# First terms of a depthwise sum on ScalarE instead of VectorE, with VectorE's other sums in the reverse order

## Chip, cores, metric

One core of one Trainium2 chip. The metric is the device time of one execution in microseconds (us), the median of several. A ratio is the mean time of one kernel's fast runs over that of the other kernel's fast runs of the same rounds, so it is not quite the ratio of the medians quoted beside it. Intervals are 95%.

## The reference

Input `x` is 2 x 256 x 128 x 128 in fp32. Layer 0 normalises it by groups and adds a block whose expensive part are three branches of a deformable depthwise 3x3 convolution (dilations 1, 9 and 12): each of nine taps reads the image at a bilinearly interpolated place, and the taps are summed with one weight per channel and tap. Then come LayerNorm, GELU, a 1x1 convolution and an MLP. Layer 1 is a group norm and a 3x3 convolution with ternary weights.

```python
def _deform_dw(x, offset, w, pad, dil):
    ...
    sampled = _bilinear(x, py, px)
    wk = w.reshape(C, K)
    return jnp.einsum('bckhw,ck->bchw', sampled, wk)
...
def _branch(x, w_off, w_def, lw, lb, pad, dil):
    off = _conv(x, w_off, pad, dil)
    y = _deform_dw(x, off, w_def, pad, dil)
    return jax.nn.gelu(_ln2d(y, lw, lb), approximate=False)
```

## The kernel before

The changed stage is sampling. One *unit* is two input rows of one branch; each unit has two halves of 128 channels, and I call such a half a *sample*. For a sample:

- TensorE multiplies 14 tiles `xs` of the padded image with the interpolation weights `A`, two tiles per PSUM buffer `pm` (four buffers).
- ScalarE copies each `pm` into `ev` (two buffers), for all nine taps.
- VectorE builds `A` of the next but one unit from `hy` and `hx` (loads of 384 KB each, three buffers), and adds `weight x ev` of each tap to rows of a ring, one ring for each branch. The first tap that touches a row writes it (the *first term*, `tensor_scalar`), the others add to it (the *sums*, `scalar_tensor_tensor`).

A *row of taps* is the three taps kx = 0, -1, 1 of one ky. The sample's two input rows feed ring rows y - ky x dilation, so the rows of taps of one unit write different ring rows in the two wide branches, and overlapping ones at dilation 1. Nearly all ring rows are begun by ky = -1 (752 of the 788 first terms). Between the samples the work on finished rows (transposes, LayerNorm, GELU, MLP: the *tail*) is interleaved in a fixed program order.

```python
def accumulate(u, c, ev, ky):                       # one row of taps
    ...
    for kx in (0, -1, 1):
        ...
            dst = ring[:, c, y % n_ring : y % n_ring + j - i, x0:x1]
            src = ev[:, tap * RI + i : tap * RI + j, u0 : u0 + x1 - x0]
            if new:
                ...                                 # frees the ring rows' last owner
                pin(nc.vector.tensor_scalar(dst, src, w, None, ALU.mult))
                begun.update((b, br, c, y + m) for m in range(j - i))
            else:
                pin(nc.vector.scalar_tensor_tensor(dst, src, w, dst, ALU.mult, ALU.add))
            i = j

def sample(u, c):
    ...
    ev = pool.tile([P, 9 * RI, NT * CI], F32, name="ev", tag="ev", bufs=2)
    for T in range(0, NT, 2):
        ...
        pm = psum.tile([P, 2, 256], F32, name="pm", tag="pm", bufs=4)
        for j in range(2):
            pin(nc.tensor.matmul(pm[:, j, 0:n], lhsT=xts[b, Rt][T + j][...], rhs=A[...], ...))
        pin(nc.scalar.copy(ev[...], pm[...]))
    if c == KC - 1:
        prepare(u + 2)                              # builds A of unit u + 2, loads for u + 3
    for ky in kys:                                  # -1, 0, 1
        accumulate(u, c, ev, ky)
```

## Time and profile before

| | before |
|---|---|
| median of 4 runs | 7882.2 us (7873.1 to 7889.1) |
| stages in the profile | first stage to 980 us, sampling to 6670 us, last stage to 7903 us |
| VectorE first terms | 788 instructions, 748 of them 128x256 |
| VectorE sums | 6272 instructions |

The lines are in the prediction below. Two ways of counting are added here, because the experiments use them. In steady stretches the program repeats every 12 samples; I take the time from the first copy of sample 100 to that of sample 364 of the first image, and between the same places of the second (484 to 772 of all 796), 46 repeats together. It is 88.21 us for a repeat in this profile and 88.35 us in a second one taken later. And the records of the granted clock show TensorE at half its clock in pieces of 3413 ns and more; in the steady stretches (1450 to 3600 and 4250 to 6400 us) there are 68 such pieces, 78 in the second profile.

### The profile page before, as it was taken

To read this page: it belongs to the slowest core of one execution; us is meant where nothing else is said; L and a number is where in the kernel's file an instruction comes from. 1 tells how busy PE (TensorE), PEld (TensorE's weight loads), DVE (VectorE), ACT (ScalarE), POOL (GpSimd) and SP (SyncE) were. 2 spreads that over 40 slices of the span, in tenths; PEclk is the share of its full clock that TensorE was granted. 3 is DMA by queue.
4 is the path that set the end of the run, shared out by engine and by line. 5 is a ranking of instruction groups with operands and counts; after the bars stand their busy time and mean duration, and the time that the engine had idled before them with its cause. 6 is when DMAs were issued, how large, how long until landed. Compare 5 with 4: busy or idle time off the path is not lost. (4 is left out here: it accounts for less than half of the span.)

```text
span 7903.1 us, 115440 instructions
## 1 busy us (share of the span) xinstructions
PE 7101.1 (90%) x37984; PEld 5421.9 (69%) x37984; DVE 6400.1 (81%) x13680; ACT 4514.7 (57%) x9350; POOL 715.1 (9%) x1292
## 2 busy tenths in 40 slices
PE   5999887899999999899988989999998999699999
PEld 2555577777887777777777777877787777344444
DVE  6666578888999889988688898898889986577776
ACT  1344355666666666667655666666666666333232
POOL 0000000111111111111100111111111111000000
PEclk9999889999999999999999999999999999799999
DMA  8767799999999999998689999999999995222121
GB/s 280 215 187 195 187 229 243 235 247 246 244 240 249 242 243 241 246 243 224 192 233 243 239 248 245 243 240 245 249 240 244 243 242 162 74 74 78 63 82 48
DMA packets 1011327, 1652.66 MB, mean 209 GB/s; under 512 B 120800, under 2 KB 573200, under 8 KB 1006360
## 3 DMA queue, kind: packets, MB, share of 16 engines
q1 hardware_dynamic: 993304, 1611.57, 76.3%
q10 hardware_dynamic: 17408, 33.56, 1.3%
q8 instruction: 304, 4.98, 0.3%
q14 instruction: 311, 2.55, 0.1%
HBM read 1376.69 MB, written 268.09 MB: 208 GB/s over the span
## 5 line engine op out<-in xcount | busy, mean ns | idle before, releaser
L759 PE MATMUL pm<-A,xs 128*128 128x180 f32 (+2 forms) x22288 | 3638.8, 319 | 578.6 <-ACT ev L768 551.2
L759 PEld LDWEIGHTS pm<-A,xs 128*128 128x128 f32 x22288 | 3431.7, 196 | 791.6 <-ACT ev L768 652.0
L768 ACT COPY ev<-pm 128x360 f32<-128x360 f32 (+2 forms) x5572 | 2283.3, 456 | 1517.3 <-DVE ring L733 751.3
L733 DVE SCALAR_TENSOR_TENSOR ring<-ev,defw,ring 128x256 f32<-128x256 f32 (+5 forms) x6272 | 2786.9, 463 | 212.5 <-ACT ev L768 43.2
L689 DVE TENSOR_TENSOR A<-hy,hx 128x768 f32<-128x768 f32 x1130 | 1018.7, 946 | 343.5 <-DMA hx<-hats 170.7
L487 ACT ACTIVATE T<-T,rs 128x256 f32<-128x256 f32 x1280 | 663.8, 595 | 3.3 <-POOL rs L483 3.2
L1083 PE MATMUL pc<-cring,signs 128*128 128x512 bf16 x2304 | 522.8, 386 | 56.1 <-DVE signs L971 23.6
L480 POOL TENSOR_SCALAR rs<-mv 128x4 f32<-128x4 f32 x320 | 108.0, 337 | 5108.0 <-DVE mv L478 4133.9
L1083 PE MATMUL pc<-cring,sums 128*128 128x512 bf16 x2304 | 510.3, 380 | 0.0
L446 PE MATMUL hp<-T,w 128*128 128x512 f32 x1024 | 490.7, 604 | 7.8 <-ACT T L565 7.8
L476 DVE BATCH_NORM_STATS2 st<-T 128x6 f32<-128x256 f32 x1280 | 446.9, 412 | 23.2 <-ACT T L468 23.2
L203 PE MATMUL pz<-wz,xa 128*128 128x486 f32 x1024 | 461.2, 584 | 4.3 <-DVE zr L210 4.3
L1083 PEld LDWEIGHTS <-signs 128*128 128x128 bf16 x2304 | 227.5, 99 | 340.7 <-issue 46.2
L446 PE MATMUL h<-hT,w 128*128 128x512 f32 x1024 | 460.1, 592 | 0.0
L1083 PEld LDWEIGHTS <-sums 128*128 128x128 bf16 x2304 | 225.4, 98 | 274.4 <-DVE sums L1143 0.2
L499 PEld LDWEIGHTS zc<-ident,T 128*128 128x128 f32 x2560 | 342.0, 156 | 98.2 <-issue 61.5
L515 ACT ACTIVATE T<-zc,bb,bw 128x512 f32<-128x512 f32 x384 | 278.5, 779 | 227.8 <-PE zc L499 226.8
L499 PE MATMUL zc<-ident,T 128*128 128x128 f32 x2560 | 384.5, 297 | 19.6 <-ACT T L487 14.1
L1067 ACT CAST cring<-D 128x2048 bf16<-128x2048 f32 x128 | 243.3, 1902 | 222.9 <-PE pc L1083 152.2
L482 POOL TENSOR_TENSOR rs<-rs,mhalf 128x4 f32<-128x4 f32 x320 | 369.6, 1155 | 0.0
L468 ACT COPY T<-tp 128x512 f32<-128x512 f32 x640 | 345.2, 599 | 38.0 <-PE tp L466 37.3
L1091 ACT ACTIVATE o<-xl,l1b 128x1024 f32<-128x1024 f32 x64 | 73.5, 1149 | 506.9 <-DMA out_x<-o 431.7
(120 smaller groups left out, 5768.7 us busy)
## 6 DMA issues: line engine op xcount, KB each, us to landing
hy<-hats SPq DMA_DIRECT2D x1114, 384.0 KB, 6.4
hx<-hats SPq DMA_DIRECT2D x1114, 384.0 KB, 7.3
xs<-table SPq DMA_DIRECT2D x1876, 128.0 KB, 4.4
g12d<-T SPq DMA_DIRECT2D x128, 512.0 KB, 7.1
other<-g12d SPq DMA_DIRECT2D x128, 512.0 KB, 10.1
hats<-hb SPq DMA_DIRECT2D x192, 240.0 KB, 4.3
hats<-hb SPq DMA_DIRECT2D x192, 192.0 KB, 3.3
xl<-x1d SPq DMA_DIRECT2D x56, 640.0 KB, 4.1
```

The costliest lines, as they stand in the source:

```text
L203: nc.tensor.matmul(pz[:, 0:NZ], lhsT=xt[:, c, r, :], rhs=k["wz"][:, c, :], start=c == 0, stop=c == KC - 1,)
L446: nc.tensor.matmul(out, lhsT=w, rhs=v, start=i == 0, stop=i == n - 1)
L468: nc.scalar.copy(Tv[:, 2 * h : 2 * h + 2, :].rearrange("p j c -> p (j c)"), tp)
L476: pin(nc.vector.bn_stats(st[:, j, :], Tv[:, j, :]))
L482: nc.gpsimd.tensor_tensor(rs[:, 0, :], rs[:, 0, :], mhalf[:, 0:NB4], ALU.pow)
L487: nc.scalar.activation(Tv[:, j, :], Tv[:, j, :], AF.Identity, scale=rs[:, 0, j : j + 1], bias=rs[:, 1, j : j + 1],)
L499: nc.tensor.transpose(zc[:, j * P : (j + 1) * P], Tv[:, j, c * P : (c + 1) * P], ident)
L689: nc.vector.tensor_tensor(dst, hy[:, i0:i1].rearrange("p i t w -> p t i w"), hx[:, i0:i1].rearrange("p i t w -> p t i w"), ALU.mult,)
L733: nc.vector.scalar_tensor_tensor(dst, src, w, dst, ALU.mult, ALU.add)
L759: nc.tensor.matmul(pm[:, j, 0:n], lhsT=xts[b, Rt][T + j][:, c * P : (c + 1) * P], rhs=A[:, m0:m1, AO + (T + j) * CI : AO + (T + j + 1) * C ...
L768: nc.scalar.copy(ev[:, m0:m1, T * CI : (T + 2) * CI].rearrange("p m (t j) -> p t m j", j=CI), pm[:, :, 0:n].rearrange("p t (m j) -> p t m ...
L1083: nc.tensor.matmul(pc[:, bank, :], lhsT=w[:, m * P : (m + 1) * P], rhs=xc[:, i, k, t * JC : (t + 1) * JC, kx : kx + W], start=j == 0, stop ...
```

## The change

The intent is to take work off VectorE, which shares the stage's bound, and give it to ScalarE, which is idle for a third of it. As the sums of ky = -1 now need what another engine writes, they go last, so that ScalarE is done by then.

```diff
-        def accumulate(u, c, ev, ky):
+        def accumulate(u, c, ev, kys):
...
+            sums = {ky: [] for ky in kys}
+            for ky in kys:
...
-                        pin(nc.vector.tensor_scalar(dst, src, w, None, ALU.mult))
+                            pin(nc.scalar.mul(dst, src, w))
...
-                        pin(
-                            nc.vector.scalar_tensor_tensor(
-                                dst, src, w, dst, ALU.mult, ALU.add
-                            )
-                        )
+                            sums[ky].append((dst, src, w))
...
+            for ky in reversed(kys):
+                for dst, src, w in sums[ky]:
+                    pin(nc.vector.scalar_tensor_tensor(dst, src, w, dst, ALU.mult, ALU.add))
...
-            for ky in kys:
-                accumulate(u, c, ev, ky)
+            accumulate(u, c, ev, kys)
```

More of the change, by code (lines that the diff above doesn't have):

```diff
@@ L695, in build @@
             )
-        def accumulate(u, c, ev, ky):
+        def accumulate(u, c, ev, kys):
             b, Rt, br = units[u]
             dil = DILS[br]
-            i0, i1 = valid(Rt, br, ky)
             ring = k["rings"][br]
             n_ring = RINGS[br]
-            for kx in (0, -1, 1):
-                tap = (ky + 1) * 3 + kx + 1
-                x0, x1 = max(0, -REACH - kx * dil), min(W, W + REACH - kx * dil)
-                u0 = x0 + kx * dil + REACH
-                w = defw[:, c, br * 9 + tap : br * 9 + tap + 1]
-                i = i0
-                while i < i1:
-                    y = Rt * RI - REACH - ky * dil + i
-                    new = (b, br, c, y) not in begun
-                    j = i + 1
-                    while (
-                        j < i1
-                        and (y + j - i) % n_ring
-                        and ((b, br, c, y + j - i) not in begun) == new
-                    ):
-                        j += 1
-                    dst = ring[:, c, y % n_ring : y % n_ring + j - i, x0:x1]
-                    src = ev[:, tap * RI + i : tap * RI + j, u0 : u0 + x1 - x0]
-                    if new:
-                        assert kx == 0
-                        for m in range(y, y + j - i):
-                            owner = owners.get((br, m % n_ring // R))
-                            while owner and owner != (b, br, m // R) and owner not in tail.read:
-                                tail.advance()
-                            owners[br, m % n_ring // R] = b, br, m // R
-                        pin(nc.vector.tensor_scalar(dst, src, w, None, ALU.mult))
-                        begun.update((b, br, c, y + m) for m in range(j - i))
-                    else:
-                        pin(
-                            nc.vector.scalar_tensor_tensor(
-                                dst, src, w, dst, ALU.mult, ALU.add
-                            )
-                        )
-                    i = j
@@ new lines, in accumulate @@
+            sums = {ky: [] for ky in kys}
+            for ky in kys:
+                i0, i1 = valid(Rt, br, ky)
+                for kx in (0, -1, 1):
+                    tap = (ky + 1) * 3 + kx + 1
+                    x0, x1 = max(0, -REACH - kx * dil), min(W, W + REACH - kx * dil)
+                    u0 = x0 + kx * dil + REACH
+                    w = defw[:, c, br * 9 + tap : br * 9 + tap + 1]
+                    i = i0
+                    while i < i1:
+                        y = Rt * RI - REACH - ky * dil + i
+                        new = (b, br, c, y) not in begun
+                        j = i + 1
+                        while (
+                            j < i1
+                            and (y + j - i) % n_ring
+                            and ((b, br, c, y + j - i) not in begun) == new
+                        ):
+                            j += 1
+                        dst = ring[:, c, y % n_ring : y % n_ring + j - i, x0:x1]
+                        src = ev[:, tap * RI + i : tap * RI + j, u0 : u0 + x1 - x0]
+                        if new:
+                            assert kx == 0
+                            for m in range(y, y + j - i):
+                                owner = owners.get((br, m % n_ring // R))
+                                while owner and owner != (b, br, m // R) and owner not in tail.read:
+                                    tail.advance()
+                                owners[br, m % n_ring // R] = b, br, m // R
+                            pin(nc.scalar.mul(dst, src, w))
+                            begun.update((b, br, c, y + m) for m in range(j - i))
+                        else:
+                            sums[ky].append((dst, src, w))
+                        i = j
```

## The prediction

> **What bounds the kernel now.** I read the page first, then the table of stretches, the waits, the timeline of one repeat, and the groups by shape. The page's busy times and slices (198 us each) show that the stage in which all changed lines run, sampling, lasts from slice 5 to slice 33, about 1000 to 6670 us.
>
> ```profile
> PE 7101.1 (90%) x37984; PEld 5421.9 (69%) x37984; DVE 6400.1 (81%) x13680; ACT 4514.7 (57%) x9350; POOL 715.1 (9%) x1292
> ...
> PE   5999887899999999899988989999998999699999
> ...
> DVE  6666578888999889988688898898889986577776
> ACT  1344355666666666667655666666666666333232
> ...
> DMA  8767799999999999998689999999999995222121
> ```
>
> TensorE, VectorE and the DMA engines all stand near nine tenths there, ScalarE near seven. The table of stretches gives figures (columns: length, busy us and count of PE, PEld, DVE, ACT, POOL, granted clock, DMA share, GB/s), first for a steady stretch, then for the first rows of the second image:
>
> ```profile
> 5000.00:6000.00 1000.00, 920.07 (x5137) 791.23 (x5136) 895.31 (x2041) 679.88 (x1462) 129.02 (x228) 0.97 0.94 244
> ...
> 4100.00:4200.00 100.00, 80.03 (x495) 75.97 (x494) 85.79 (x184) 57.02 (x131) 5.83 (x12) 0.95 0.98 250
> ```
>
> Three resources within 3% of each other cannot all be the bound at once: they take turns. The waits of the sampling stage (us in total, times, longest) say how they hand over.
>
> ```profile
> PE pm L759 <- ACT ev L768: 550.5, 300, 6.5
> ...
> ACT ev L768 <- DVE ring L733: 751.3, 343, 8.0
> ACT ev L768 <- PE pm L759: 443.1, 352, 3.7
> ...
> DVE A L689 <- DMA hx<-hats: 158.6, 115, 6.2
> DVE A L689 <- PE pm L759: 142.5, 68, 8.4
> DVE ring L729 <- ACT ev L768: 105.6, 74, 4.3
> ```
>
> Read together: `ev` has two buffers, so ScalarE may not copy sample s out of PSUM before VectorE has finished the sums of sample s-2; while it waits, four `pm` banks fill and TensorE stops. That is the 550 us. In other places VectorE waits for TensorE or a load.
>
> The steady part repeats every 88.7 us (12 samples: 6 units of two channel halves). In one repeat, 5024.9 to 5113.6, TensorE has just four gaps, and these are them in the timeline (start, us, what, then [idle before <- releaser]):
>
> ```profile
> 5028.95 2.10 PE L759 MATMUL pm<-A,xs 128*128 128x180 f32 x12 [0.43 <-ACT ev L768]
> ...
> 5058.25 3.78 PE L759 MATMUL pm<-A,xs 128*128 128x180 f32 x12 [3.30 <-ACT ev L768]
> ...
> 5070.91 2.10 PE L759 MATMUL pm<-A,xs 128*128 128x180 f32 x12 [0.43 <-ACT ev L768]
> ...
> 5079.32 3.58 PE L759 MATMUL pm<-A,xs 128*128 128x180 f32 x12 [2.99 <-ACT ev L768]
> ```
>
> ScalarE's own rows before the last three show waits of 3.63, 1.85 and 2.37 us for VectorE's sums. So VectorE sets the end only from about 5050 (where it starts building `A` just as TensorE finishes with the old one) to 5079. From 5079 until the next stall near 5147 TensorE runs on with no more than 0.43 us lost at one place, and VectorE's first terms there (eight of twelve) are hidden behind it. The four at 5053.11, 5057.54, 5065.96 and 5074.56 are exposed.
>
> **What the skill says.** "VectorE: DVE Perf Modes", section on the perf-mode tier table: an fp32 `tensor_scalar` in SBUF gets 2x, a two-tensor op 1x. The trace agrees: for the same 256 elements 342 ns against 483 ns, a difference of 141 ns where 128 cycles saved at the page's 0.96 GHz are 133. So the change takes VectorE's cheapest ring write away, not its dearest. "ScalarE: Activation LUTs", section "What ACT_TABLE_LOAD costs": 186 ns + 0.833 ns per element, about 93 ns more per [128,1] operand. The trace agrees: two operands and 256 elements give 585 against 595 ns (L487); one operand and 512 elements give 706 against 716 (L538). For the new form, one operand and 256 elements, it gives 492; I add the same 10 ns and a little for waiting on the engine's own last copy: 520 ns, an estimate from that page. "Perfetto Trace Analysis", section on Scalar/DVE operations: if VectorE is saturated, moving work to ScalarE may pay. VectorE's 895 of 1000 us against ScalarE's 680 is that situation, but only for a third of each repeat.
>
> **The change part by part.** The groups by shape (count | busy us, mean ns | idle before):
>
> ```profile
> L768 ACT COPY ev<-pm 128x360 f32<-128x360 f32 x4788 | 2037.6, 472 | 1320.7 <-DVE ring L733 688.0 <-PE pm L759 388.8 <-PE hp L446 12.5
> L733 DVE SCALAR_TENSOR_TENSOR ring<-ev,defw,ring 128x256 f32<-128x256 f32 x2832 | 1366.7, 483 | 110.3 <-ACT ev L768 43.2
> ...
> L487 ACT ACTIVATE T<-T,rs 128x256 f32<-128x256 f32 x1280 | 663.8, 595 | 3.3 <-POOL rs L483 3.2
> ...
> L729 DVE TENSOR_SCALAR ring<-ev,defw 128x256 f32<-128x256 f32 x748 | 255.8, 342 | 113.0 <-ACT ev L768 112.6
> ```
>
> Removed: 788 first terms from VectorE (748 of them this wide). From the start of one to the start of the next sum is 0.38 us (5053.11 to 5053.49), so about 788 x 0.38 = 299 us of VectorE's queue. On the path are four per repeat: 4 x 0.38 = 1.5 us of 88.7, or 1.7%. Steady stretches are roughly 1450 to 3650 and 4300 to 6450 us, 4350 us together, hence 49 repeats: 49 x 1.5 = 74 us. At the start of each image I count nothing: between 4000 and 4300 VectorE stands 39 us waiting for `hx` and the DMA share is up to 0.98. At each image's end few rows are begun at all.
>
> Added: 788 x 0.52 = 410 us on ScalarE (4515 to about 4925). By the built programs' order each stands just after the seven copies of its sample and waits for nothing but these, so it falls into the time in which ScalarE waits for VectorE or TensorE next. In the stretch that counts these waits were 3.6, 1.9 and 2.4 us, and where TensorE leads 3.6 us before sample 5024.94. I put 0 on the path. No activation table load is added: three before and after.
>
> Moved: the sums of the lowest row of taps (`ky` = -1, to which nearly all first terms belong) come last. With three or six other sums of some 0.48 us first, VectorE has 1.4 to 2.9 us before it needs the 0.52 us write. The removed 0.38 us is thus not replaced by a wait. The sums keep number and sizes, and TensorE's order is instruction for instruction the same. Sum: 7885 - 74, say **7812 us**, 0.9% less.
>
> **The rivals.** (1) VectorE is the bound throughout: all 299 us come off, 7586 us. For it: 89.5% busy and 751 us of ScalarE waiting for it. Against: its own waits of over 500 us in this stage, and TensorE without gaps for two thirds of a repeat. (2) The DMA takes it back: share 0.94 and 243 GB/s against at most 250 GB/s in stretches where loads are the visible wait. A repeat shorter by 1.7% needs 247. For it: `hx` already ends 115 waits, and buffers that come free sooner only queue the loads sooner. Then a third to all of the 74 us goes: 7835 to 7885. (3) ScalarE becomes the bound: it would rise from 68 to about 75% in steady stretches; where it interleaves tail work with copies, 0.5 us per sample could delay TensorE. If half the samples lost 0.2 us, 796 x 0.5 x 0.2 = 80 us would cancel the gain: about 7890. Against: TensorE's gaps from ScalarE all begin with VectorE or lie behind a 3.6 us idle time of ScalarE.
>
> **Range and chances.** The mechanism removes at most what lies on the path, so 74 is nearer a ceiling than a middle of the steady part; the start of the images, and repeats in which more first terms are exposed than in the one I read, can add some 40 to 60 us. Down to 7750 on that side. On the other, rivals 2 and 3 reach 7875. Faster by over 2% means under 7728, twice my saving: 5%. Slower by over 2% would need ScalarE to become the path: 2%.
>
> **What would show it.** Right: VectorE's first-term group gone; a ScalarE group of 788 at 500 to 540 ns; VectorE busy near 6130; ScalarE near 4920; the repeat about 87.2 us; TensorE's wait for `ev` down by 60 to 100 us; no wait of the sums for the first terms. Wrong: the wait for `hx` grown by some 70 us (rival 2), TensorE's wait for `ev` grown while ScalarE's for VectorE shrank (rival 3), or TensorE's wait nearly halved (rival 1). A new write much over 520 ns, or a repeat in which VectorE leads for longer than 29 us, would make the number wrong.

## The result, and the profile after

The changed kernel takes 7756.2 us (median of 4, 7735.4 to 7761.0) against 7882.2 us, ratio 0.984 [0.982, 0.986]: 126 us less. This is within the range (7750 to 7875), 6 us from its lower end, under the 2% of "faster", and 52 us more gain than the 74 us predicted.

The page's busy times of the changed kernel, then its row of the steady stretch (length, busy us and count of PE, PEld, DVE, ACT, POOL, clock, DMA share, GB/s):

```profile
PE 7065.1 (91%) x37984; PEld 5377.1 (69%) x37984; DVE 6136.4 (79%) x12892; ACT 4818.2 (62%) x10138; POOL 708.7 (9%) x1292
```

```profile
5000.00:6000.00 1000.00, 929.10 (x5308) 799.91 (x5308) 877.58 (x1960) 753.59 (x1656) 131.45 (x232) 0.98 0.96 250
```

VectorE lost 264 us and 788 instructions, ScalarE gained 304 us. In the steady thousand TensorE does 171 more matmul records in the same time (a product of the sampling is two records), VectorE is less busy, and the DMA moves 250 GB/s where it moved 244. The groups by shape (count | busy us, mean ns | idle before):

```profile
L740 DVE SCALAR_TENSOR_TENSOR ring<-ev,defw,ring 128x256 f32<-128x256 f32 x2832 | 1355.2, 480 | 248.7 <-ACT ev L771 174.2 <-DVE ring L740 0.9
...
L733 ACT ACTIVATE ring<-ev,defw 128x256 f32<-128x256 f32 x748 | 378.8, 509 | 23.6
```

The first term costs ScalarE 509 ns where it cost VectorE 342, and ScalarE hardly waits for it. The waits of the sampling stage, one fence for each engine (us, times, longest):

```profile
PE pm L762 <- ACT ev L771: 437.1, 276, 7.9
```

```profile
ACT ev L771 <- DVE ring L740: 461.3, 253, 8.7
ACT ev L771 <- PE pm L762: 393.8, 236, 5.3
```

```profile
DVE A L689 <- DMA hx<-hats: 227.0, 151, 7.3
DVE ring L740 <- ACT ev L771: 175.2, 89, 5.8
DVE A L689 <- PE pm L762: 139.2, 66, 5.8
...
DVE ring L740 <- ACT ring L733: 14.4, 9, 3.0
```

TensorE waits 113 us less, ScalarE waits 290 us less for VectorE, and VectorE waits more for loads and for ScalarE's copies (175.2 us where two lines of the kernel before had 105.6 and 32.9): it comes earlier. For the first terms themselves it waits 14 us. TensorE's gaps in one repeat (start, us, what, [idle before]):

```profile
4998.66 2.10 PE L762 MATMUL pm<-A,xs 128*128 128x180 f32 x12 [0.42 <-ACT ev L771]
...
5026.64 2.10 PE L762 MATMUL pm<-A,xs 128*128 128x180 f32 x12 [1.98 <-ACT ev L771]
...
5038.26 2.10 PE L762 MATMUL pm<-A,xs 128*128 128x180 f32 x12 [0.84 <-ACT ev L771]
...
5046.31 2.10 PE L762 MATMUL pm<-A,xs 128*128 128x180 f32 x12 [2.64 <-ACT ev L771]
```

The two large gaps stand at the same two samples of the repeat (the 8th and the 11th of twelve) as before, 2.0 and 2.6 us instead of 3.3 and 3.0. And something that I had overlooked before: behind them twelve records (six products) take 2.10 us, while in the kernel before they took 3.78 and 3.58 us behind the large gaps. The clock records show why: a half-clock piece of 3413 ns begins at 5058.47 us and one at 5078.95 us, and none in this repeat of the changed kernel. Where the gain arises, from the two profiles:

| part of sampling | before | after | gain |
|---|---|---|---|
| samples 0 to 100 (start of image 1) | 645.3 | 623.6 | 21.7 |
| 100 to 364, steady | 1945.0 | 1892.2 | 52.8 |
| 364 to 412 (end of image 1) | 326.9 | 331.2 | -4.3 |
| 412 to 484 (start of image 2) | 505.5 | 496.3 | 9.2 |
| 484 to 772, steady | 2112.6 | 2059.7 | 52.9 |
| 772 to 796 (end) | 153.2 | 153.0 | 0.2 |

The first stage, which the change doesn't touch, differs by 20 us between the two profiles; a second profile of the kernel before (below) lies between. That is spread, and not part of the table.

### The profile page after: what moved, and what is told of

It is laid out like the page before. It is cut to its first block, busy times and chain, and to the rows that moved or that the text cites. A ratio compares the mean times of both kernels' runs of the same rounds, so it can differ in the third digit from the quotient of the medians.

```text
span 7751.0 us, 115301 instructions
## 1 busy us (share of the span) xinstructions
PE 7065.1 (91%) x37984; PEld 5377.1 (69%) x37984; DVE 6136.4 (79%) x12892; ACT 4818.2 (62%) x10138; POOL 708.7 (9%) x1292
## 5 line engine op out<-in xcount | busy, mean ns | idle before, releaser
L740 DVE SCALAR_TENSOR_TENSOR ring<-ev,defw,ring 128x256 f32<-128x256 f32 (+3 forms) x6272 | 2774.5, 462 | 359.7 <-ACT ev L771 175.2
L771 ACT COPY ev<-pm 128x360 f32<-128x360 f32 (+2 forms) x5572 | 2235.8, 455 | 1131.6 <-DVE ring L740 462.9
L733 ACT ACTIVATE ring<-ev,defw 128x256 f32<-128x256 f32 (+1 forms) x788 | 392.2, 503 | 24.1
L499 PEld LDWEIGHTS zc<-ident,T 128*128 128x128 f32 x2560 | 325.9, 151 | 97.5 <-issue 61.5
L499 PE MATMUL zc<-ident,T 128*128 128x128 f32 x2560 | 368.7, 289 | 20.1 <-ACT T L487 13.9
```

Of the source, the lines that this page charges most:

```text
L499: nc.tensor.transpose(zc[:, j * P : (j + 1) * P], Tv[:, j, c * P : (c + 1) * P], ident)
L733: pin(nc.scalar.mul(dst, src, w))
L771: nc.scalar.copy(ev[:, m0:m1, T * CI : (T + 2) * CI].rearrange("p m (t j) -> p t m j", j=CI), pm[:, :, 0:n].rearrange("p t (m j) -> p t m ...
```

## The experiments

Eleven kernels ran (no run has the number e11). All results were correct except in the one made wrong. This table holds what the traces of all give; it is used below. *Block* is the time that VectorE takes for the first terms and sums of 12 samples, from the start of the first to the end of the last, as the sum of the median blocks of the three branches times four. *Repeat* is the mean of 46, *half-clock* the number of half-clock pieces in the steady stretches.

| kernel | ratio to before [95%] | block, us | repeat, us | half-clock |
|---|---|---|---|---|
| before (two profiles) | 1.001 [0.999, 1.002] (e8) | 51.3 | 88.21, 88.35 | 68, 78 |
| changed | 0.984 [0.982, 0.986] | 46.9 | 85.91 | 41 |
| e1 order only | 0.992 [0.990, 0.993] | 49.8 | 87.18 | 62 |
| e2 ScalarE only | 0.987 [0.985, 0.988] | 46.7 | 86.37 | 52 |
| e3 no first terms | 0.981 [0.980, 0.983] | 46.7 | 85.72 | 40 |
| e4 first terms twice on VectorE | 1.023 [1.021, 1.025] | 56.0 | 91.40 | 85 |
| e5 before, stalls filled | 0.997 [0.996, 0.999] | as before | 87.20 | 5 |
| e6 changed, stalls filled | 0.982 [0.981, 0.983] | as changed | 85.34 | 0 |
| e7 first terms twice on ScalarE | 0.988 [0.986, 0.989] | as changed | 86.00 | 35 |
| e9 before, sums spread | 0.967 [0.965, 0.969] | 42.8 | 84.12 | 29 |
| e10 changed, sums spread | 0.962 [0.960, 0.963] | 39.6 | 83.19 | 20 |
| e12 before, filled elsewhere | 1.005 [1.002, 1.008] | as before | 88.91 | 23 |

**e1: the order alone.** The first terms stay on VectorE.

```diff
-                            pin(nc.scalar.mul(dst, src, w))
+                            pin(nc.vector.tensor_scalar(dst, src, w, None, ALU.mult))
```

> The first terms stay on VectorE, only its sums run in the reverse order of rows of taps. My theory (the gain is VectorE time taken off the stretches in which VectorE leads, plus shorter TensorE stalls that less often end in a half-clock window): nothing is taken off VectorE, so the ratio to the kernel before is 0.998 to 1.002, VectorE stays near 6400 us busy and the half-clock windows in the steady stretches stay near 68. Rival (the order itself frees rows of the ring or shortens dependent sums): a part of the 1.6% is seen here, 0.995 or less.

Measured: 7829.2 us, ratio 0.992. My expectation was wrong and the rival's range came true: reversing the sums alone gives half of the gain, though not one instruction leaves VectorE. The timeline tells which of the rival's two reasons it was. A first term and the eight sums behind it, in the kernel before:

```profile
5037.82 0.35 DVE L729 TENSOR_SCALAR ring<-ev,defw 128x256 f32<-128x256 f32 x1
5038.20 3.77 DVE L733 SCALAR_TENSOR_TENSOR ring<-ev,defw,ring 128x238 f32<-128x238 f32 x8
```

and in e1:

```profile
5037.04 0.35 DVE L733 TENSOR_SCALAR ring<-ev,defw 128x256 f32<-128x256 f32 x1
5037.31 3.76 DVE L740 SCALAR_TENSOR_TENSOR ring<-ev,defw,ring 128x256 f32<-128x256 f32 x8
```

Before, the sum behind the first term adds to the rows that this has just written, and starts 0.38 us after it. In e1 it belongs to other rows and starts after 0.27 us, while the first term's 0.35 us are not over. The same is seen among the sums over two rows (about 250 elements, 0.47 to 0.48 us each): the median step between two starts is 0.38 to 0.40 us where the next one has other rows, and 0.50 to 0.52 us where it adds to the rows just written. So here an instruction starts some 0.08 us before the end of the one in front, but 0.03 us after it if it needs that one's result: about 0.12 us later. e1 removes one dependent neighbour per sample, 51.3 - 49.8 = 1.5 us per repeat, of which 1.1 us arrive in the time. I took this as the new theory and tested it in e9.

**e2: ScalarE alone.** The sums keep their order.

```diff
-            for ky in reversed(kys):
+            for ky in kys:
```

> The first terms go to ScalarE, but VectorE's sums keep the order of before, so the sums that need the first terms come first. My theory: where VectorE leads it is behind ScalarE by more than a sample, so the first term is there already; only where VectorE waits for ScalarE's copies (about once in 12 samples, where TensorE leads) does it wait some 0.5 us more. So 0.984 to 0.988 of before, almost the whole gain. Rival (the order is needed): a wait of 0.5 us takes the place of the removed 0.38 us in most samples, the ratio is 0.995 or more and VectorE's wait for ScalarE's first terms is over 100 us.

Measured: 7786.2 us, ratio 0.987, as expected within its range. VectorE's waits:

```profile
DVE A L689 <- DMA hx<-hats: 257.0, 161, 6.7
DVE ring L740 <- ACT ring L733: 180.3, 86, 6.2
...
DVE ring L740 <- ACT ev L771: 47.3, 18, 4.4
```

Of the rival, one sign came (a wait for first terms of over 100 us) and the other did not (a ratio of 0.995 or more): VectorE waits for first terms 86 times, about once or twice per repeat, not in all 796 samples, in places where the changed kernel waits 89 times for the copies in front of them (175 us). The sum of both waits is 227.6 us against 189.6. So the order's own purpose, to hide ScalarE's latency, is worth some 0.3% (0.987 against 0.984 in other rounds; 0.46 us per repeat). It also shows that the two parts do not add up: the order shortens a block by 1.5 us and the move by 4.7, but both together by 4.4, because without the first term there is no dependent neighbour left for the order to break up, and at dilation 1 the fourth sum now waits for both engines and starts 0.07 us later than in e3, which has no first terms.

**e3: no first terms anywhere** (wrong, the rings are cleared once).

```diff
-                            pin(nc.scalar.mul(dst, src, w))
...
+            for ring in k["rings"]:
+                nc.vector.memset(ring, 0.0)
```

> Wrong result on purpose: the first terms are left out on both engines (the ring is cleared once), all else as in the changed kernel. My theory (ScalarE's 392 us stand beside other work): the same time as the changed kernel, 0.982 to 0.986 of before. Rival (ScalarE's new work takes part of the gain back): clearly less, 0.978 or lower.

Measured: 7748.2 us, ratio 0.981 [0.980, 0.983], between my range (from 0.982) and the rival's (0.978 or lower). The changed kernel's interval [0.982, 0.986] just overlaps. Per repeat e3 is 0.2 us shorter. So ScalarE's 392 us of new work cost at most a few tenths of a per cent, and in steady stretches nearly nothing.

**e4: each first term twice on VectorE.**

```diff
                         pin(nc.vector.tensor_scalar(dst, src, w, None, ALU.mult))
+                        pin(nc.vector.tensor_scalar(dst, src, w, None, ALU.mult))
```

> The kernel before with each first term written twice by VectorE (the same values), 788 more instructions of 0.38 us, 299 us in all. My theory: 4 to 6 of 12 are exposed and the longer stalls meet more half-clock windows, 1.5 to 2.5 us for each of the 49 repeats, 1.010 to 1.016 of before, with more than 68 half-clock windows in the steady stretches. Rival (VectorE is the bound throughout): 1.03 to 1.04. Rival (only TensorE or the DMA counts): 1.003 or less.

Measured: 8074.6 us, ratio 1.023, beyond my range and below the rival's. 4.7 us more block per repeat lengthen the repeat by 3.1. VectorE's work is exposed to two thirds around the kernel before (what comes through the clock included), not to one third. Its half-clock pieces rise to 85.

**e5, e6: useless products inside the stalls.** At the 8th and 11th sample of twelve, the fourth pair of products is computed four times more (three times in e6).

```diff
+                again = 4 if T == 6 and count[0] % 398 % 12 in (7, 10) else 0
-                for j in range(2):
+                for j in [0, 1] * (1 + again):
```

> The kernel before with useless TensorE work where it stalls anyway: at samples 7 and 10 of every 12 the fourth pair of products is computed four times more (some 2.4 us, the same values), just ahead of the stall of about 3 us. VectorE's and ScalarE's work is as before. My theory (a stall of about 3 us brings a half-clock window of 3.4 us on TensorE, which then takes some 1.7 us more): the half-clock windows in the steady stretches fall from 68 to under 25, the time falls to 0.988 to 0.995 of before though work was added. Rival (the clock windows don't lie on the path): 1.000 or more.

> The changed kernel with the same fill, three times instead of four (1.8 us, as its stalls are shorter, 2.2 and 2.5 us in the mean). My theory: of the 41 half-clock windows in the steady stretches most go, up to 26 times 1.7 us are won, the fill costs some of it where the stall is shorter than the fill: 0.978 to 0.985 of before, so at best a little faster than the changed kernel. Rival: slower than the changed kernel by the fill, 0.986 or more.

Measured: e5 7867.4 us, 0.997 [0.996, 0.999]; e6 7746.8 us, 0.982. The row of the first steady stretch, before and in e5:

```profile
1450.00:3600.00 2150.00, 1960.54 (x11126) 1690.57 (x11126) 1930.25 (x4405) 1465.20 (x3169) 279.11 (x487) 0.97 0.93 243
```

```profile
1450.00:3600.00 2150.00, 2056.13 (x12067) 1777.63 (x12066) 1948.16 (x4451) 1472.13 (x3217) 283.38 (x496) 1.00 0.95 247
```

The clock is full, 0.97 before and 1.00 here, and adding work made the kernel a little faster. So the half-clock pieces do lie on the path, against the rival, but for less than I expected: 1.1 us per repeat for some 68 pieces less in 46 repeats, 0.7 us for each piece, net of what the fill itself may cost. At the ends of the images, where the fill meets no stall, it costs: 15.3 us more than before at the end of the first. e6 wins 0.6 us per repeat on the changed kernel.

**e7: each first term twice on ScalarE.**

```diff
                             pin(nc.scalar.mul(dst, src, w))
+                            pin(nc.scalar.mul(dst, src, w))
```

> The changed kernel with each first term written twice by ScalarE (the same values), 788 more instructions of 0.50 us, 392 us more on ScalarE. My theory: ScalarE still has idle time in every sample that counts, 0.984 to 0.990 of before. Rival (ScalarE is now on the path): half of the 392 us or more shows, 1.008 or more.

Measured: 7788.4 us, 0.988 [0.986, 0.989], within my range. 392 us more on ScalarE cost some 0.4%; 0.1 us per repeat in steady stretches, the rest at the starts and ends of the images.

**e8: the kernel before again.**

> The kernel before, unchanged, for a second profile on this chip: 1.000. It tells how much of the 20 us by which the first, unchanged stage differed between the two first profiles, and of the difference at the image starts, is the chip's spread: if a part of the profile's gain was spread, this profile starts sampling near 960 us and not near 980.

Measured: 7895.5 us, 1.001. Sampling starts at 971.5 us, against 981.8 in the first profile before and 961.4 in the one after: the first stage's time is spread of 10 us either way. Samples 0 to 100 take 646.5 us, like the first profile's 645.3, so the gain at the image start is real.

**e9, e10: the sums spread.** The next sum is taken from the rows of taps that do not touch the rows just written, the longest queue first; e9 keeps the first terms on VectorE, e10 is the changed kernel with that order.

```diff
-                            sums[ky].append((dst, src, w))
+                            sums[ky].append((set(range(y, y + j - i)), dst, src, w))
...
-            for ky in reversed(kys):
-                for dst, src, w in sums[ky]:
-                    pin(nc.vector.scalar_tensor_tensor(dst, src, w, dst, ALU.mult, ALU.add))
+            last = set()
+            while any(sums.values()):
+                ky = max(
+                    (ky for ky in kys if sums[ky]),
+                    key=lambda ky: (not sums[ky][0][0] & last, len(sums[ky]), ky),
+                )
+                last, dst, src, w = sums[ky].pop(0)
+                pin(nc.vector.scalar_tensor_tensor(dst, src, w, dst, ALU.mult, ALU.add))
```

> From the first eight runs: a VectorE sum starts 0.38 us after the previous one when that wrote other rows, and 0.50 to 0.52 us after it when it adds to the same rows. Reversing the order alone put a sum of other rows behind the first term and won 0.8%. Here all first terms stay on VectorE, and its sums are taken in turn from the rows of taps, so that as few as possible follow one that wrote the same rows. Theory (the step between dependent instructions is what the order changed): VectorE's block for one sample falls from 4.15 to about 3.45 us in the two wide branches, its queue is shorter by some 500 us, the time is 0.973 to 0.982 of before, more than the change gave although nothing moves to ScalarE. Rival (the reversal helped for another reason, such as rows that are ready earlier for TensorE): 0.99 to 1.00.

> The changed kernel with its sums taken in turn from the rows of taps, as in e9. Theory: VectorE's block falls from 3.76 to about 3.2 us in the two wide branches, then TensorE leads nearly everywhere and little is left to win: 0.968 to 0.979 of before, fewer than 25 half-clock windows in the steady stretches. Rival (the change has already taken all that VectorE exposes): 0.983 or more.

Measured: e9 7634.3 us, 0.967; e10 7591.3 us, 0.962. Both beat the expectations. VectorE's block of eight sums in e9:

```profile
5023.93 0.35 DVE L733 TENSOR_SCALAR ring<-ev,defw 128x256 f32<-128x256 f32 x1
5024.19 3.13 DVE L745 SCALAR_TENSOR_TENSOR ring<-ev,defw,ring 128x256 f32<-128x256 f32 x8
```

The same eight sums take 3.1 instead of 3.8 us. The group in e10 shows it as a sum:

```profile
L745 DVE SCALAR_TENSOR_TENSOR ring<-ev,defw,ring 128x256 f32<-128x256 f32 x2832 | 1236.5, 478 | 257.9 <-ACT ev L776 233.9
```

2832 times 478 ns are 1354 us, but the group was busy for 1236.5 us: the instructions lie over each other. In the kernel before, 2832 times 483 ns are 1368 and the group was busy for 1366.7. A group of one shape doesn't show what lies over a neighbour of another shape, so here are the sums of all shapes, before:

```profile
L733 DVE SCALAR_TENSOR_TENSOR ring<-ev,defw,ring 128x256 f32<-128x256 f32 (+5 forms) x6272 | 2786.9, 463 | 212.5 <-ACT ev L768 43.2
```

and in e10:

```profile
L745 DVE SCALAR_TENSOR_TENSOR ring<-ev,defw,ring 128x256 f32<-128x256 f32 (+5 forms) x6272 | 2471.5, 457 | 289.9 <-ACT ev L776 239.2 <-ACT ring L733 25.1
```

Before, 4% of their 2904 us lie over each other, in e10 14% of 2866. In e9 the waits between sums are still there (4460 of the 6272 sums wait for VectorE's own semaphore, 4476 in e1), for the sum two or three places ahead, and cost nothing; so it is the need of the result just being written that costs, not the wait as such. e9 takes twice the change's gain without moving anything to ScalarE, which the rival (rows ready earlier for TensorE) does not explain. e10 is the best version: 2.2% less than the changed kernel (0.962 over 0.984, from different rounds).

**e12: the fill of e5 at samples where TensorE has no gap** (the 3rd and 5th of twelve; `in (2, 4)`).

> A control for e5: the same useless products at samples 2 and 4 of every 12, where TensorE leads and has no stall. Theory: each of the some 130 fills of 2.4 us lies on the path, 200 to 320 us, 1.025 to 1.040 of before. If it were as cheap as in e5 (0.997), the fill of e5 would tell nothing of the clock.

Measured: 7935.0 us, 1.005, far under my range. 4.8 us more TensorE work per repeat, in a stretch in which it runs without gaps, lengthen the repeat by 0.6 us only. With the half-clock pieces gone from 68 or 78 to 23, worth some 0.7 us per repeat by e5, about 1.3 of the 4.8 us were exposed (an estimate). The trace shows where the rest went: the stall at the 8th sample fell from 3.3 to 0.7 us in the mean of all repeats, while the one at the 11th (2.9 before, 2.7 here) hardly changed. TensorE's wait for ScalarE's copies (1000 to 6650 us), 550.5 us before, became

```profile
PE pm L761 <- ACT ev L770: 388.8, 234, 6.3
```

So TensorE had been working ahead there, towards its next long stall.

## Why the prediction was right or wrong

- **Removed work and its size: right.** 788 first terms left VectorE, at 0.37 us each (block 4.4 us per 12), predicted 0.38. VectorE's busy time was to be 6130 us and is 6136. ScalarE's new write was to take 520 ns and takes 509.
- **ScalarE's load: too high.** It was to be busy for about 4920 us and was for 4818. The prediction added 788 times 0.52 us; in the trace ScalarE's next instruction starts 0.09 us (median) before the end of such a write, and each adds about 0.39 us to the busy time (304 us in all).
- **ScalarE not on the path: right** (e3, e7), within some tenths of a per cent. Rival 3 falls. So does rival 1: of its 299 us 126 came.
- **"The four at 5053.11, 5057.54, 5065.96 and 5074.56 are exposed": this step failed, and it is the term of the sum that was mis-sized.** It gave 1.5 us per repeat; measured are 2.3 to 2.4, a repeat of 85.9 us where 87.2 was named, and TensorE's wait fell by 113 us where 60 to 100 were. I had read "TensorE has no gap" as "TensorE leads". e12 contradicts: TensorE could take 4.8 us more there for about a quarter of the price. e1 and e4 show that around the kernel before some 70% of a small change of VectorE's work arrives in the time (1.1 of 1.5 us, 3.1 of 4.7), and the changed kernel, whose cut is larger, gets 2.4 of 4.4 (the clock's share included in all). The share sinks with the size of the cut: e9 gets 4.2 of 8.5 and e10 5.1 of 11.7. VectorE's waits for `hx` (1000 to 6400 us) grow along with it: 156.1 us before, 226.4 in the changed kernel, 295.2 in e9, 349.2 in e10.
- **Half clock: not in the sum.** The stalls that became shorter led to a half-clock restart less often, 41 instead of 68 or 78. Comparing e6 with e5, both nearly without such pieces, the change is worth 1.9 us per repeat; so about 0.5 of the 2.4 us come through the clock (an estimate: the two fills are not equally long), and 1.9 us are five first terms of 0.37 us rather than four.
- **Starts of the images: wrong, counted as nothing.** They gave 22 and 9 us. The range did name them, with repeats in which more first terms are exposed, as worth 40 to 60 us more; the two together brought 52 by the medians, so the lower end held for the reasons given for it. I had called these stretches bound by loads, but a load is issued only when VectorE has freed a buffer, so VectorE's time is in that loop too. Which wait hands it on was not tested by itself.
- **Rival 2: its sign came, its effect did not.** The waits for `hx` grew by 68 us, as the prediction said rival 2 would show. The gain stayed, because VectorE only came to the loads earlier. The ceiling of 250 GB/s was wrong: e10 moves 257 GB/s in its first steady stretch.
- **"The removed 0.38 us is not replaced by a wait": right** (14 us in all), and the order is what saves about 38 us of waits (e2). That the order does nothing else held in the changed kernel, but only because the first term was gone (e1 against e2).
- **Two readings were off, and nothing hung on them.** TensorE, VectorE and the DMA stood at 92, 89.5 and 94% in the row shown, so within 5% of each other and not 3%. And the trace shows two table loads of ScalarE, before and after, not three; none was added, as predicted.
- Taken together, from the profiles: 46 repeats times 2.3 us (106), image starts 31, ends -4, makes 133 us; the medians differ by 126.

## What to carry to other kernels

An engine without gaps need not lead: it may be working ahead of what the others can use; put a little work there, or take a little away, and see how much arrives. On VectorE, before moving instructions to another engine, look at the steps between starts: accumulating into the same rows in consecutive instructions cost more here than an order in which neighbours are independent, and reordering alone gave twice what moving the first terms gave. Here stalls of some 3 us on TensorE cost more than their length where a half-clock piece followed (some 0.7 us for each, e5), so a cut that shortens stalls can return more than the time it removes.

## What the Trainium skill lacked or had wrong

- "VectorE: DVE Perf Modes", section on the DRAIN, says the next op does not start until the pipe is empty and that chaining without semaphores changes nothing; its rules say to minimise the op count, not the waits. Here fp32 sums of about 250 elements start 0.38 to 0.40 us apart where neighbours are independent and 0.50 to 0.52 us where one adds to what the other wrote (e1, e9: an instruction of 0.46 to 0.48 us). Order, at the same op count and with waits kept, gave 3.3%. The same section adds that an op that is not held starts earlier, but neither it nor the section that it points to names a gain for accumulations.
- "Perfetto Trace Analysis", section on Scalar/DVE operations, has the write-acknowledgement half of an instruction's fixed overhead overlap with the next instruction; it doesn't say that this is lost for a dependent neighbour (which starts 0.12 us later here).
- "TensorE: Matmul & The Clock Gate" has a half-clock window of about 3.4 us after an idle one. The trace agrees (3413 ns pieces). What it lacks is how often shorter stalls bring it: stalls of over 1 us at the 8th and 11th sample were 3.3 and 3.0 us long in the mean before and 67 of 96 had a half-clock restart; with 2.2 and 2.5 us it was 41 of 98. In the steady stretches of all 13 profiles a half-clock piece (running at the end of the gap, or beginning within 3.5 us of it) went with 20 of 428 gaps of 1 to 2 us, with 301 of 547 of 2 to 3 us, and with all 56 of 4 us and more. One such piece cost about 0.7 us of time here (e5).
- "ScalarE: Activation LUTs", in its rules for authors, sends multiplications to VectorE. Here ScalarE took 509 ns for what VectorE did in 342, and the kernel was 1.3 to 1.6% faster, as "Perfetto Trace Analysis" allows where VectorE is saturated.
